# The order of the second expert turn worked out on the chip, and the last layer norm of half the rows placed among the short expert slots

## The chip, the cores and the metric

The kernel runs on one core of a Trainium2 chip. The number that is compared is the device time of the whole program in microseconds (us); each run has one time, and a kernel's time is the median of its runs. A profile is one further execution, recorded by the hardware profiler: its span runs from the first to the last instruction.

The core has TensorE (PE, matmuls; "PEld" is its weight load), VectorE (DVE), ScalarE (ACT), GpSimd (POOL) and SyncE (SP). SP and POOL issue nearly all of the DMAs here. An engine takes its instructions strictly in order: one that waits holds all that stand behind it.

## The reference

One attention layer and one mixture of experts, each followed by a layer norm, on x of shape (4, 1024, 256): 4 batch elements of 1024 tokens.

```python
x = layernorm(x + attention(x))                     # 16 heads of 16, causal
scores = (x @ router_w.T + router_b) / temp
gates  = sinkhorn(scores)                           # 3 rounds over experts and tokens of an element
topk_vals, topk_idx = top_k(gates, 2)
topk_gates = topk_vals / (topk_vals.sum(-1) + 1e-8)
g = relu(einsum('btd,edf->btef', x, wg))            # 8 experts, 256 -> 512
p = einsum('btd,edf->btef', x, wp)
all_out = einsum('btef,efd->bted', g * p, wo)       # 512 -> 256
x = layernorm(x + sum of the 2 chosen outputs, each times its gate)
```

For the given inputs the router gives the 8 experts 476, 472, 478, 516, 533, 481, 598 and 542 pairs (token, expert) from the first two elements, and 952, 937, 945, 1020, 1051, 995, 1219 and 1073 from all four (worked out from the reference).

## The kernel before

The attention of element b runs beside the projections of element b + 1 and the routing (`route`) of element b - 1. Routing is sparse: each pair is written by an indirect DMA into a list in DRAM, `pairs`, which has a region for each expert (`scatter`, L848). `base` holds each expert's next free row. An entry has the row to gather, the row to add to, and the gate.

The experts then run in *slots*. The first turn is 8 slots of 512 rows, one for each expert in the order 0 to 7; it needs only the pairs of the first three elements and starts before the last element is routed. The second turn is 8 more slots of 512 rows, the experts in the order 7 to 0, with the next 512 pairs of each; it waits for the last pairs. Its first slot takes the split weights of the slot before it (`second[0].like = first[-1]`), as that is the same expert. Then come `SURE` = 3 short slots of 256 rows for what is left over, with the expert and the place of the list read from a table that `lay_out` made; each such number is a register load on SP (`value`). Were more than three short slots filled, a conditional block would run the rest; here three are filled, so it is skipped.

What a slot does: `pairs_of` loads its entries, `gather` has POOL fetch 4 (or 2) blocks of 128 rows of x1 by indirect DMA into `xg`, `rows` turns them over on PE and splits them into a high and a low part (`split`: ACT makes the high part, DVE the low one), `weights` loads wg, wp and wo (512 KB each) on SP, `halves` splits them, and `slot` does the matmuls, three for each product (`mm3`). At its end ACT scales each 128-row block by its gate into `eo`, and POOL adds it to DRAM, `results`, by an indirect DMA that accumulates (L1039). The adds of a slot wait for the adds of the slot before it to have landed, since two experts may add to one row (`added`, `after`). `results` holds x1 from the start, so x + expert_out is there when all adds have landed. `begin(keys, n)` prepares slot n in pieces while slot n - 1 runs.

After the last slot everything is waited for. Then SP loads all of `results` in 8 pieces of 512 rows (L1255), and each piece gets its layer norm: DVE takes mean and variance (L1269, L1270), POOL makes the factor and the offset (L1272 to L1276), and the rows are scaled by ACT (first 5 pieces, L1279) or by DVE (the last `DZ` = 3, L1287) and stored (L1258).

The order of the instructions of each engine is made by a scheduler when the program is built, from the order of the calls and from a timeline of its own.

Of the kernel before, what the change touches and what calls it, by code (L numbers as in the profile page):

```python
# [9 lines left out]
F32 = mybir.dt.float32  # L10
# [13 lines left out]
DZ = 3  # L24
HB = 6
SURE = 3
# [15 lines left out]
def kernel(  # L42
# [40 lines left out]
    REGION = BT + SR  # L83
    NOVER = (2 * BT - 4 * ER + 2 * (SR - 1)) // SR
# [101 lines left out]
    def split(hi, lo, src, sub=None):  # L186

        nc.scalar.copy(hi, src)  # L188
        (sub or nc.vector).tensor_tensor(lo, src, hi.bitcast(F32), ALU.subtract)  # L189
# [495 lines left out]
    def route(b):  # L685
# [141 lines left out]
        nc.vector.tensor_tensor(base, base, ps[:, NE : NE + E], ALU.add)  # L827
        if b == B - 2:
            nc.vector.tensor_tensor(base, base, floor, ALU.max)
# [36 lines left out]

    def lay_out():
# [36 lines left out]
        nc.vector.tensor_copy(tables["filled"], upto[:, E - 1 :])  # L904
# [3 lines left out]
    def value(r, s, top):  # L908
        return nc.values_load(
            tables["slots"][0:1, r, s : s + 1], engines=[mybir.EngineType.SP], min_val=0, max_val=top,  # L910
            skip_runtime_bounds_check_because="worked out on the chip from counts that add up to 2 * B * T",
        )
# [10 lines left out]
    class Slot:  # L923


        def __init__(self, which, s):
            self.which, self.s, self.name = which, s, f"{which}_{s}"
            self.rows = SR if which == 2 else ER
            self.blocks = self.rows // P
            self.raw, self.hl = [None] * 3, [None] * 3  # L930
            self.like = None
# [3 lines left out]
    def pairs_of(k):  # L935
        if k.which == 2:
            row = value(1, k.s, NLIST - SR)
            k.ent = const.tile([P, k.blocks, 4], I32, name=f"ent_{k.name}")
            nc.sync.dma_start(
                out=k.ent, in_=pairs[bass.ds(row, SR)].rearrange("(p j) w -> p j w", j=k.blocks)  # L940
            )
            return
        if k.which not in lists:
# [6 lines left out]
            if not k.which:  # L950
                apart("pairs", "early", ins, ("last",))
        k.ent = lists[k.which][:, k.s]

    def gather(k):
        k.xg = early.tile([P, ER // P, C], F32, tag="xg", name=f"xg{k.name}", bufs=XG)
        for j in range(k.blocks):
# [3 lines left out]
            )  # L960
            if not k.which:
# [9 lines left out]
    def weights(k, i):  # L971

        if k.like is not None:
            return
        if k.which == 2:
            if i == 0:
                k.e = value(0, k.s, E - 1)
            rows_e = bass.ds(k.e, 1)
        else:
            rows_e = slice(k.s, k.s + 1)  # L980
# [4 lines left out]
    def halves(k, i):  # L985
        if k.like is not None:
            k.hl[i] = k.like.hl[i]
            return
# [16 lines left out]
    def slot(k, between):  # L1005
# [3 lines left out]
        for f in range(NFC):  # L1009
# [14 lines left out]
            split(hh, hlo, r)  # L1024
            hs.append((hh, hlo))
            next(between, None)
            if k in first[E - 3 : E - 1]:
                places.give(1.0)
        mine = []
# [85 lines left out]
    second = [Slot(1, e) for e in reversed(range(E))]  # L1115
    second[0].like = first[-1]
# [80 lines left out]
    for gen in (finish(B - 1, (0,), alone=True), route(B - 1), lay_out()):  # L1197
        drain(gen)
    filled = nc.values_load(
        tables["filled"][0:1, 0:1], min_val=0, max_val=NOVER,  # L1200
# [26 lines left out]
    def run(keys, given=()):  # L1227
        drain(begin(keys, 0, given))
        for n, key in enumerate(keys):
            slot(key, begin(keys, n + 1, given))  # L1230
            if key is first[E - 2]:
                places.until(f"S{B - 1}")

    run(first + second + further[:SURE], (0,))
# [7 lines left out]


    zp = ctx.enter_context(tc.tile_pool(name="zp", bufs=1))
    y_rows = out.rearrange("b t c -> (b t) c")
    zs = {}

    def rows_of(of, i, cut=slice(0, BPQ)):

        return of[i * QC : (i + 1) * QC].rearrange("(p n) c -> p n c", p=P)[:, cut]  # L1250

    def load_z(i):
        z = zp.tile([P, CC, FF], F32, tag="z", name=f"z{i}", bufs=BT // QC)
        z = zs[i] = z.rearrange("p k f -> p (k f)").rearrange("p (n c) -> p n c", c=C)
        nc.sync.dma_start(out=z, in_=rows_of(results, i))  # L1255

    def store_z(i, z, cut=slice(0, BPQ)):
        nc.sync.dma_start(out=rows_of(y_rows, i, cut), in_=z[:, cut])  # L1258

    n_z = BT // QC  # L1260
    rest = []
    for i in range(n_z):
        load_z(i)
    for i in range(n_z):
        z = zs.pop(i)
        mv = small.tile([P, BPQ, 2], F32, tag="mv", name=f"mv_f{i}", bufs=2)
        for j in range(BPQ):
            st = small.tile([P, 6], F32, tag="bnst", name=f"bnst_f{i}_{j}")
            nc.vector.bn_stats(st, z[:, j, :])  # L1269
            nc.vector.bn_aggr(mv[:, j, :], st)  # L1270
        rstd = small.tile([P, BPQ], F32, tag="rstdz", name=f"rstd_f{i}", bufs=4)
        nc.gpsimd.tensor_scalar_add(rstd, mv[:, :, 1], EPS_LN / 4)  # L1272
        nc.gpsimd.tensor_tensor(rstd, rstd, neg_half, ALU.pow)
        off = small.tile([P, BPQ], F32, tag="offz", name=f"off_f{i}", bufs=4)
        nc.gpsimd.tensor_tensor(off, mv[:, :, 0], rstd, ALU.mult)
        nc.gpsimd.tensor_scalar(off, off, -1.0, None, ALU.mult)  # L1276
        if i < n_z - DZ:
            for j in range(BPQ):
                nc.scalar.activation(  # L1279
                    z[:, j, :], z[:, j, :], AF.Identity, bias=off[:, j : j + 1], scale=rstd[:, j : j + 1]  # L1280
                )
            store_z(i, z)
        else:
            rest.append((i, z, rstd, off))
# [84 lines left out]
```

## Time and profile before

| | |
|---|---|
| three runs | 1086.51, 1090.79, 1091.84 us; median 1090.79 |
| the profiled execution | 1095.9 us, span 1094.2 us, mean granted TensorE clock 0.957 |
| PE busy | 975.8 us, 89% of the span |
| DVE, ACT, POOL busy | 734.9, 625.4 and 479.1 us |
| DMA | 119.67 MB, 109 GB/s over the span |

The share of PE is an average over stages. Busy time by stage, from the view by windows: in 700 to 860 us (first turn) PE is busy for 150.2 of 160 us, in 860 to 900 us for 25.5 of 40, in 900 to 1020 us (second turn) for 119.3 of 120, in 1020 to 1060 us (end of the second turn and short slots) for 36.5 of 40, and in 1060 to 1094 us for none. The gap at 860 us lies between the turns, where the list of pairs has to be complete; the 34 us at the end are the last adds and the layer norm.

### The profile page before, as it was taken

The numbers are of one execution on the slowest core, as the hardware profiler recorded it, in microseconds if no ns is written. First come the engines' busy times: TensorE is split into PE (matmuls) and PEld (weight loads), VectorE is DVE, ScalarE is ACT, GpSimd is POOL, SyncE is SP. The second block draws the span as 40 slices with busy tenths as digits, with TensorE's granted clock in tenths as the row PEclk, the third lists the DMA queues.
The fourth block names the chain that finished last, engine by engine and source line by source line (L and its number), as shares of the span: only waits on it lengthen the run. The fifth ranks groups of instructions, "written<-read, shape, count | busy, mean of one in ns | idle before, by whom it ended". The sixth has DMA issues, their size and how long they took to land.

```text
span 1094.2 us, 18114 instructions
## 1 busy us (share of the span) xinstructions
PE 975.8 (89%) x6436; PEld 608.2 (56%) x6436; DVE 734.9 (67%) x1622; ACT 625.4 (57%) x1314; POOL 479.1 (44%) x543
## 2 busy tenths in 40 slices
PE   6689999999999999989999996899999399999970
PEld 4555433455544455543444443488888288888860
DVE  4767787888888778787757882286686145555536
ACT  3445666765665755666656663656565145555533
POOL 6177511022352632552223215427557655554535
PEclk9889999999989999999999998999999699999985
DMA  6574420231240330333143220357555345656537
GB/s 245 165 213 121 117 86 18 76 117 33 95 121 17 107 114 5 127 80 98 47 102 98 46 70 2 99 174 186 141 125 123 69 109 113 172 113 164 123 36 307
DMA packets 71363, 119.67 MB, mean 109 GB/s; under 512 B 16416, under 2 KB 43040, under 8 KB 70880
## 3 DMA queue, kind: packets, MB, share of 16 engines
q1 hardware_dynamic: 48544, 81.76, 24.3%
q0 software_dynamic: 20672, 36.41, 15.5%
q8 instruction: 53, 0.87, 0.3%
q10 hardware_dynamic: 2048, 0.27, 0.2%
q14 instruction: 46, 0.38, 0.1%
HBM read 82.52 MB, written 35.60 MB: 108 GB/s over the span
## 4 chain that ended last, share of the span: by engine, by line
PE 74%; DMA 7%; DVE 6%; ACT 5%; SPq 4%; issue 2%; POOL 2%; another core or an unknown queue 1%; ACTq 0%; POOLq 0%; DVEq 0%
PE y L436 12%; PE s L351 11%; PE sT L456 10%; SPq L336 3%; PE gp L197 3%; PE gp L196 3%; PE gp L195 3%; PE eo L197 3%; PE eo L196 3%; PE eo L195 3%; PE po L625 3%; PE lp L197 2%; PE lp L196 2%; ACT pT L467 2%; PE lp L195 2%
## 5 line engine op out<-in xcount | busy, mean ns | idle before, releaser
L467 ACT ACTIVATE pT<-sT 128x512 f32<-128x512 f32 (+1 forms) x608 | 327.1, 575 | 180.8 <-PE sT L456 129.2
L372 DVE TENSOR_REDUCE mx<-s 128x1 f32<-128x384 f32 (+3 forms) x352 | 216.6, 633 | 36.2 <-PE s L368 35.1
L351 PE MATMUL s<-ks,qs 96*128 96x512 bf16 (+3 forms) x768 | 212.4, 333 | 19.4 <-DMA ks<-parts 10.8
L456 PE MATMUL sT<-qs,ks 98*128 98x512 bf16 (+3 forms) x768 | 215.5, 330 | 9.0 <-ACT pT L467 6.9
L381 DVE TENSOR_REDUCE mx<-s 128x1 f32<-128x512 f32 x256 | 171.4, 682 | 47.6 <-PE s L351 47.1
L474 POOL TENSOR_SCALAR_AFFINE_SELECT pT<-pT 128x512 f32<-128x512 f32 x112 | 70.7, 638 | 254.9 <-ACT pT L467 250.4
L436 PE MATMUL y<-pT,va 128*32 128x512 f32 (+3 forms) x1536 | 169.2, 503 | 4.4 <-ACT pT L467 3.1
L1039 POOL DMA_INDIRECT results<-eo,ents x64 | 107.2, 1674 | 82.6 <-ACT eo L1038 65.4
L351 PEld LDWEIGHTS <-qs 96*128 96x128 bf16 x768 | 70.8, 99 | 120.3 <-issue 89.7
L456 PEld LDWEIGHTS <-ks 98*128 98x128 bf16 x768 | 69.8, 99 | 89.6 <-issue 57.4
L848 POOL DMA_INDIRECT pairs<-ent,so_i x64 | 67.8, 1060 | 75.9 <-ACT pT L467 57.5
L368 PE MATMUL s<-mask,ident_b 128*128 128x128 bf16 (+2 forms) x352 | 87.1, 248 | 0.0
L1020 DVE TENSOR_TENSOR relu<-relu,lp 128x512 f32<-128x512 f32 x64 | 43.7, 683 | 60.1 <-ACT relu L1019 30.6
L195 PE MATMUL eo<-wh,hh 128*128 128x256 f32 x280 | 80.5, 289 | 0.9 <-ACT eo L1038 0.6
L957 POOL DMA_INDIRECT xg<-x_rows,ents x64 | 65.1, 1017 | 33.6 <-issue 16.1
L196 PE MATMUL eo<-wl,hh 128*128 128x256 f32 x280 | 79.0, 284 | 0.0
L189 DVE TENSOR_TENSOR wl<-w,wh 128x512 fp32r<-128x512 f32 x108 | 69.3, 684 | 14.3 <-ACT wh L188 13.8
L197 PE MATMUL eo<-wh,hl 128*128 128x256 f32 x280 | 77.7, 284 | 0.0
L1019 ACT ACTIVATE relu<-gp 128x512 f32<-128x512 f32 (+1 forms) x76 | 42.7, 563 | 59.6 <-PE gp L197 49.9
L436 PEld LDWEIGHTS y<-pT,va 128*32 128x32 f32 x1536 | 31.8, 108 | 64.6 <-issue 46.5
L195 PE MATMUL gp<-xh,wh 128*128 128x512 f32 (+1 forms) x176 | 65.0, 376 | 2.1 <-ACT xh L188 1.2
L196 PE MATMUL gp<-xl,wh 128*128 128x512 f32 (+1 forms) x176 | 65.6, 374 | 0.0
(213 smaller groups left out, 1849.0 us busy)
## 6 DMA issues: line engine op xcount, KB each, us to landing
ks<-parts SPq DMA_DIRECT2D x90, 128.0 KB
w<-in_wg_dram SPq DMA_DIRECT2D x18, 512.0 KB
w<-in_wp_dram SPq DMA_DIRECT2D x18, 512.0 KB
w<-in_wo_dram SPq DMA_DIRECT2D x18, 512.0 KB
qs<-parts SPq DMA_DIRECT2D x66, 128.0 KB
parts<-lv POOLq DMA_DIRECT2D x12, 384.0 KB
parts<-lv POOLq DMA_DIRECT2D x24, 192.0 KB
xh<-in_x_t_dram SPq DMA_DIRECT2D x8, 512.0 KB
```

Source lines behind the costliest of these rows:

```text
L195: nc.tensor.matmul(ps, lhsT=sh, rhs=mh, start=(i == 0), stop=False)
L196: nc.tensor.matmul(ps, lhsT=sh, rhs=ml, start=False, stop=False)
L197: nc.tensor.matmul(ps, lhsT=sl, rhs=mh, start=False, stop=(i == n - 1))
L351: nc.tensor.matmul(ps, lhsT=q(h, half)[:NROW, t * P : (t + 1) * P], rhs=k(h, kc)[:NROW, :w], start=first, stop=last,)
L368: nc.tensor.matmul(each[:, :, w - P :], lhsT=ident_b, rhs=mask.unsqueeze(1).to_broadcast([P, m, P]), start=False, stop=True,)
L372: nc.vector.tensor_reduce(mx_of[:, half, h0 : h0 + m, t], each, AX.X, ALU.max)
L381: nc.vector.tensor_reduce(mx_of[:, kc, h, t : t + 1], ps, AX.X, ALU.max)
L436: nc.tensor.matmul(acc[g, qc][SLOT * h : SLOT * (h + 1), lo:], lhsT=va[b % 2][:, kb, at : at + SLOT], rhs=pT[:, h, lo:], start=(kb == 0), ...
L456: nc.tensor.matmul(st[:, h % m * w : (h % m + 1) * w], lhsT=k(h, kb // BPQ)[: NROW + 2, kb % BPQ * P : (kb % BPQ + 1) * P], rhs=q(h, qc)[: ...
L467: latest[0] = nc.scalar.activation(pT[:, h + 1 - m : h + 1, lo:], st[:, : m * w].rearrange("p (h t) -> p h t", t=w), AF.Exp, scale=scale,)
L474: diagonal[0] = nc.gpsimd.affine_select(out=block, in_=block, pattern=[[0, HG], [1, P]], compare_op=ALU.is_ge, fill=0.0, base=0, channel_m ...
L1039: ins = nc.gpsimd.indirect_dma_start(out=results[:, :], out_offset=bass.IndirectOffsetOnAxis(ap=k.ent[:, j, 1:2], axis=0), in_=eo, in_offs ...
```

## The change

Four things:

1. `order_of_second`, called in the routing of the second element, finds the expert with the fewest pairs from the first two elements and makes a table `second`: experts and list places for the second turn, in rotating order, so that this expert comes last. It also makes a flag, `again`, which sends the program into the conditional block if any expert has over 1024 pairs from these two elements. The second turn's slots now read expert and place by `value` on SP, load their entries one slot at a time, and the first of them loads and splits weights of its own.
2. An expert with at most 512 pairs from the first two elements has none of them in its second slot. So the rows of `results` of the first two elements are complete when the last but one slot of the turn has been added. `load_early` loads them, 4 pieces of 512 rows, by POOL, in the last slot of the turn, after those adds have landed.
3. Their layer norm is done by DVE beside the short slots: `center_early` (mean, variance, and the factor on POOL) for pieces 0 and 1 after the first short slot's last split, `end_early` for them and `center_early` for 2 and 3 after the second's, `end_early` for 2 and 3 after the third's. SP stores them.
4. At the end only 4 pieces are left, 2 of them scaled by ACT and `DZ` = 2 by DVE.

The conditional block, when it runs, does pieces 0 to 3 again.

```diff
-DZ = 3
+DZ = 2
...
+    EARLY = B // 2
...
         nc.vector.tensor_tensor(base, base, ps[:, NE : NE + E], ALU.add)
+        if b == EARLY - 1:
+            order_of_second()
...
+    def order_of_second():
+        few = tab("few", [E])
+        nc.vector.tensor_tensor(few, floor[:1], base[:1], ALU.subtract)
+        most, again = tab("most", [1]), tab("again", [1])
+        nc.vector.tensor_reduce(most, few, AX.X, ALU.min)
+        nc.vector.tensor_scalar(again, most, -float(ER), float(NOVER), ALU.is_lt, ALU.mult)
+        tables["again"] = again
+        nc.vector.tensor_reduce(most, few, AX.X, ALU.max)
+        nc.vector.tensor_scalar(few, few, most, None, ALU.is_equal)
+        nc.vector.tensor_tensor(few, few, rank[:1], ALU.mult)
+        nc.vector.tensor_reduce(most, few, AX.X, ALU.max)
+        seq = tab("seq", [2, E])
+        seqi = tables["second"] = small.tile([1, 2, E], I32, tag="seqi", name="seqi", bufs=1)
+        nc.vector.tensor_scalar(seq[:, 0], slot_no[:, :E], most, float(E + 1), ALU.subtract, ALU.add)
+        nc.vector.tensor_copy(seqi[:, 0], seq[:, 0])
+        nc.vector.tensor_single_scalar(seqi[:, 0], seqi[:, 0], E - 1, ALU.bitwise_and)
+        nc.vector.tensor_copy(seq[:, 0], seqi[:, 0])
+        nc.vector.tensor_scalar(seq[:, 1], seq[:, 0], float(REGION), float(ER), ALU.mult, ALU.add)
+        nc.vector.tensor_copy(seqi[:, 1], seq[:, 1])
...
-        nc.vector.tensor_copy(tables["filled"], upto[:, E - 1 :])
+        nc.vector.tensor_tensor(tables["again"], tables["again"], upto[:, E - 1 :], ALU.add)
+        nc.vector.tensor_copy(tables["filled"], tables["again"])
...
     def pairs_of(k):
-        if k.which == 2:
-            row = value(1, k.s, NLIST - SR)
+        if k.which:
+            row = value(k.table, 1, k.s, NLIST - k.rows)
...
     def weights(k, i):
-        if k.like is not None:
-            return
-        if k.which == 2:
+        if k.which:
             if i == 0:
-                k.e = value(0, k.s, E - 1)
+                k.e = value(k.table, 0, k.s, E - 1)
...
-    def slot(k, between):
+    def slot(k, between, ahead=None):
...
-            split(hh, hlo, r)
+            k.mark = split(hh, hlo, r)
...
+        if ahead is not None:
+            ahead()
...
-    second = [Slot(1, e) for e in reversed(range(E))]
-    second[0].like = first[-1]
+    second = [Slot(1, n) for n in range(E)]
...
+    def load_early():
+        for i in range(n_early):
+            z = work.tile([P, T], F32, tag="yT0", name=f"ze{i}", bufs=2) if i < 2 else work.tile(
+                [P, BPQ, C], F32, tag="x1", name=f"ze{i}", bufs=X1_BUFS
+            )
+            z = early_z[i] = z.rearrange("p (n c) -> p n c", c=C) if i < 2 else z
+            with tc.issue_after(further[0].gathered.ins):
+                ins = nc.gpsimd.dma_start(out=z, in_=rows_of(results, i))
+            for o in added:
+                after(ins, o)
+    def center_early(i):
+        mv = small.tile([P, BPQ, 2], F32, tag="mve", name=f"mv_e{i}", bufs=n_early)
+        for j in range(BPQ):
+            st = small.tile([P, 6], F32, tag="bnst", name=f"bnst_e{i}_{j}")
+            nc.vector.bn_stats(st, early_z[i][:, j, :])
+            nc.vector.bn_aggr(mv[:, j, :], st)
+        rstd = small.tile([P, BPQ], F32, tag="rstdz", name=f"rstd_e{i}", bufs=4)
+        nc.gpsimd.tensor_scalar_add(rstd, mv[:, :, 1], EPS_LN / 4)
+        nc.gpsimd.tensor_tensor(rstd, rstd, neg_half, ALU.pow)
+        early_z[i] = early_z[i], mv, rstd
+    def end_early(i):
+        z, mv, rstd = early_z[i]
+        for j in range(BPQ):
+            nc.vector.tensor_scalar(
+                z[:, j, :], z[:, j, :], mv[:, j, 0:1], rstd[:, j : j + 1], ALU.subtract, ALU.mult
+            )
+        store_z(i, z)
...
-            slot(key, begin(keys, n + 1, given))
+            slot(key, begin(keys, n + 1, given), ahead.get(n))
+            with tc.issue_after(key.mark.ins):
+                for step, i in behind.get(n, ()):
+                    step(i)
...
+    run(keys, (0,), {n: load_early}, {
+        n + 1: [(center_early, i) for i in range(half)],
+        n + 2: [(end_early, i) for i in range(half)] + [(center_early, i) for i in range(half, n_early)],
+        n + 3: [(end_early, i) for i in range(half, n_early)],
+    })
...
-    for i in range(n_z):
-        load_z(i)
-    for i in range(n_z):
+    for i in range(n_early, n_z):
+        zs[i] = zp.tile([P, BPQ, C], F32, tag="z", name=f"z{i}", bufs=n_z - n_early)
+        nc.sync.dma_start(out=zs[i], in_=rows_of(results, i))
+    for i in range(n_early, n_z):
         if i < n_z - DZ:
...
+            by_scalar(i, zs[i], "f")
         else:
...
+            rest.append((i, zs[i], *norm_z(i, zs[i], "f")))
```

`by_scalar` and `norm_z` hold what the loop over the pieces did before; `n` is the place of the last slot of the second turn, `n_early` is 4.

## The prediction, as it was made before the result was known

> **What bounds the kernel now.** By the busy shares it is PE, at 89%. By stage, from the view by windows, PE is busy for 119.31 of the 120 us of the second turn, and for nothing in the last 34 us; what the change removes lies there. The chain of waits, in order of time, says what the end is made of:
>
> ```profile
> 1054.44 3.69 DMA results<-eo,ent
> ...
> 1058.95 8.45 DMA results<-eo,ent
> ...
> 1068.04 0.34 SPq L1255
> ...
> 1068.90 6.47 DMA z<-results
> 1075.46 0.49 DVE bnst_f L1269 x2
> ```
>
> The columns are start, length, what. The adds of the second short slot are issued at 1054.44 and land, those of the third at 1058.95 and land; then the loads of `results` go out at 1068.04, and the first of two waits of DVE on them ends at 1071.33, the second at 1075.46. So the end is two queues in a row: the adds, then the layer norm. The first is read in POOL's timeline (start, length, instruction, and in brackets its idle time and who ended it):
>
> ```profile
> 1022.15 2.08 POOL L1039 DMA_INDIRECT results<-eo,ents  x1 [1.25 <-ACT eo L1038]
> 1027.90 1.54 POOL L1039 DMA_INDIRECT results<-eo,ents  x1 [3.67 <-DMA results<-eo,ents]
> 1029.75 1.01 POOL L957 DMA_INDIRECT xg<-x_rows,ent  x1 [0.30 <-PE gp L197]
> ...
> 1036.61 2.08 POOL L1039 DMA_INDIRECT results<-eo,ents  x1 [0.31 <-ACT relu L1019]
> 1043.56 1.78 POOL L1039 DMA_INDIRECT results<-eo,ent  x1 [4.87 <-ACT hh L188]
> 1047.25 1.54 POOL L1039 DMA_INDIRECT results<-eo,ent  x1 [1.91 <-ACT eo L1038]
> 1051.85 1.55 POOL L1039 DMA_INDIRECT results<-eo,ent  x1 [3.06 <-ACT relu L1019]
> 1054.44 1.54 POOL L1039 DMA_INDIRECT results<-eo,ent  x1 [1.04 <-ACT eo L1038]
> 1058.95 1.55 POOL L1039 DMA_INDIRECT results<-eo,ent  x1 [2.97 <-DMA results<-eo,ent]
> 1060.81 1.55 POOL L1039 DMA_INDIRECT results<-eo,ent  x1 [0.30 <-issue]
> ```
>
> 1022.15 is the last add of the last but one slot of the second turn, 1027.90 the first of its last slot: it waited for the former to land. 1043.56 and 1047.25 are the first short slot's, 1051.85 and 1054.44 the second's, 1058.95 and 1060.81 the third's. At 1051.85 and 1058.95 an add waits for a landing, at 1043.56, 1047.25 and 1054.44 for ACT's `eo`. The latency from an issue's end to the next slot's add is 3.06 us (1048.79 to 1051.85) and 2.97 (1055.98 to 1058.95).
>
> The DMA engines, by windows of 1 us (last columns: clock, busy share of the DMA engines, GB/s):
>
> ```profile
> 1028.00:1029.00 1.00, 1.00 (x11) 1.00 (x10) 0.00 (x0) 0.58 (x2) 1.00 (x1) 1.00 1.04 351
> ...
> 1030.00:1031.00 1.00, 1.00 (x11) 1.00 (x10) 0.82 (x3) 0.89 (x3) 0.76 (x1) 1.00 1.11 271
> ...
> 1075.00:1076.00 1.00, 0.00 (x0) 0.00 (x0) 0.54 (x2) 0.87 (x2) 0.84 (x3) 0.50 1.04 410
> ```
>
> They are full from 1026 to 1031 us with the short slots' weights, and full again in the tail. The last view is DVE's timeline:
>
> ```profile
> 1038.07 0.43 DVE L189 TENSOR_TENSOR hl<-relu,hh 128x256 fp32r<-128x256 f32 x1
> ...
> 1047.51 1.29 DVE L189 TENSOR_TENSOR wl<-w,wh 128x512 fp32r<-128x512 f32 x2 [0.46 <-issue]
> ...
> 1078.36 0.36 DVE L1270 BATCH_NORM_AGGREGATE mv_f<-bnst_f 128x2 f32<-128x6 f32 x4
> ...
> 1089.35 1.38 DVE L1287 TENSOR_SCALAR z<-z,rstd_f,off_f 128x256 f32<-128x256 f32 x4 [0.67 <-POOL off_f L1276]
> ```
>
> **The tail, minus 8.0 us.** With 4 pieces the loads and the statistics of the first four stand as they are now: the fourth's are done at 1078.72 (the third line above). POOL's fourth set starts at 1079.14, has 0.23 + 1.04 + 0.20 + 0.23 us of work, and without the next piece's add between ends at 1081.28. DVE's four scalings (1.38 us, last line) end at 1082.70, not at 1090.73: 8.03 us. Behind them lie the last store and its landing (1090.73 to the span's end, 3.47 us), as now. ACT's two pieces are done by 1079.8 (2.07 us, then 8 of the 16 scalings that take 7.97 us from 1077.81). Bounds: 7.1, if the store queue still sets the end (2.1 MB from 1077.3 at 262 GB/s, the mean of the last 6 us, lasts until 1085.3, and 1.8 us passed now between the engines' falling quiet at 1092.4 and the end), and 9, if less traffic also brings the third piece earlier and takes its 0.89 us wait away.
>
> **The adds, plus 4.8 us.** `load_early` stands on POOL where the add of 1027.90 stood, and waits for the same landing. Its four issues cost 0.88 + 3 x 0.80 = 3.3 us (the seven stores of x1 from POOL: median 0.878, then 0.787). Behind them in POOL's queue: the gather of the third short slot (2.6 us), then the four adds of the turn's last slot. These write `results`, which the loads read, so in the compiled order the first of them waits for all four loads. It went at 1027.90; now it goes when 2.1 MB have landed. First bytes come 1.5 us after the issue (store issued at 239.4, engines busy from 240.9): 1029.4. In the tail the loads had their first bytes at 1069.0, the third piece landed at 1075.46, and the fourth follows 1.3 us later at 410 GB/s: 7.7 us. Add 1.0 us for some 0.35 MB of weights still under way (0.67 MB move from 1029.4 to 1032, of which 0.26 are the gather's): 1038.1. Bounds: 1035.4 (2.1 MB at 350 GB/s) and 1040.8 (at 184 GB/s, the row of 1036 to 1040).
>
> From there I follow the queue. The four adds at a pitch of 1.95 (now 1.92 and 2.34) end at 1045.6 and land at 1048.6. First short slot: 1048.6 instead of 1043.56. Now POOL has `rstd` of pieces 0 and 1 in its order before this add and the next, 0.23 and 1.05 us each with gaps of 0.08 (1.4 us): the second add goes at 1051.9. Plus landing: 1056.5, second short slot; its second add, behind one more `rstd` step, at 1058.65; landing 1063.2, third slot; last add 1065.0 instead of 1060.81. Two `pow` of pieces 2 and 3 (2.5 us) fit into the last landing's 2.97. That is plus 4.2.
>
> DVE comes to nearly the same place by another way. Its stats of pieces 0 and 1 stand before the second short slot's work and find their data landed (wait free: 1038.5, against a first piece by about 1033). But the scaling of piece 1 waits for the `rstd` that POOL does behind the first short slot's add: 1051.6. Behind it in DVE's order stand 1.4 us of scaling, 1.41 of stats, the split of wo (1.29 us, which ran at 1047.51), then the third slot's products: the last `hl` ends at 1061.4, PE's last 15 matmuls at 0.12 us and ACT's two `eo` follow, and the last add is ready at 1065.1. If PE, idle for about 4 us by then, runs at half clock (it did at 1039 to 1042, granted clock 0.50, after being busy for 1.4 of the 3 us before), it is 1066.5. I take plus 4.8. Bounds: with the loads' landing from 1035.4 to 1040.8, plus 1.5 to plus 8. The stores of the early pieces and DVE's scaling of 2 and 3 (2.8 us after 1061.4) end before the last add lands; if not, they would be waited for, 1 us at most.
>
> The Trainium skill speaks against an early load here ("DMA: Bandwidth & Descriptors", "Issuing engines are not separate DMA queues"): a transfer issued from another engine runs on the same 16 DMA engines and interleaves with what is under way. The rows agree, since the share is 1.0 from 1026 to 1031 us; by the rule taken fully, the loads would share with all that the weights have left at 1028 (1.57 MB less the 0.76 moved since 1024), not with 0.35 MB, and the sum would be 1.3 us worse. The same page's fit for DMAs from GpSimd ("Anatomy of one DMA — SWDGE (gpsimd) path", 2.0 us plus bytes over 436 GB/s) gives as an estimate 6.8 us for the 2.1 MB, and a sum 2.5 us better; no run here shows that fit.
>
> **Between the turns, plus 0.5 us.** Now the weights of the second slot of the turn are loaded by 840 us. After the change their load stands on SP behind the entries' loads, which wait for the last pairs (864.53); entry, two register loads and the second entry (1.13 us as between the two L946 and L939 issues), so wg goes out at 866.8, wp at 867.4. On ACT and DVE their splits stand before the `xh` and `xl` of the turn's first slot, which start at 875.18 and 875.80. At 1.9 us for each 512 KB, with 3.3 us for the first (1068.04 to 1071.33), wp lands at 872.1, ACT's two casts (1.13) end at 873.2: hidden. The cover is 2.0 us. Entries for one expert instead of eight may land up to 1 us sooner, the gathers may share the engines and land 1 to 2 later. The slot's 6 extra splits and 1.5 MB take the place of those that stood there a slot later; in the turn itself, SP's register loads and entry loads run a slot ahead of the gather, and nothing waits. Bounds -1 and +13 (rival 2).
>
> **The small tables, plus 0.3 us.** 13 DVE instructions on one partition at 511 us (and one more in `lay_out`), at 0.15 us as the copies and sums of `lay_out`: 2.0 us. DVE had 13.3 busy of 20 us there and PE 18.0, so most is cover; bounds 0 and 2.2.
>
> **Sum.** -8.0 + 4.8 + 0.5 + 0.3 = -2.4 us on the profiled execution, 1095.9, so 1093.5. It lay 5.1 us over the median of the runs, 1090.79; the same difference there gives **1088.4**. All bounds on one side give 1082 and 1096 (rival 2 left out); being independent, 1084 to 1093.
>
> **Rivals.** *1, the adds catch up.* POOL's 10.9 us of idle time between 1038.69 and 1054.44 is slack: if the loads land by 1034 and the order on POOL does not matter, the adds end with ACT's `eo` as now, plus 1. Then -8.0 + 1 + 0.8: 1084.6. For it: the slack is real. Against: landing chains of 3 us stand in it, and the loads need 7.7 us alone.
>
> *2, the gap between the turns grows.* The weights that now follow the list land late, and ACT and DVE hold the gathered rows behind them. It decides once wp lands after 874.1. The price: 1.57 MB at 117 GB/s, the rate while gathers run at 870 us, from 868.3 is 13.4 us, 881.7, which is 7.6 too late; at 83 GB/s, the mean of 860 to 900, 18.9 us and 13.1 too late. In place of the 0.5 the sum is plus 4.7 to plus 10.2: 1095.5 to 1101, middle 1098. For it: SP's order is plain, and PE is idle there, so each us counts. Against: while gathers run the share of the DMA engines is only 0.3 to 0.4 (the DMA view's slices of 868 to 878 us).
>
> *3, the conditional block runs.* 22 further slots of about 10 us (1043.56 to 1051.85 to 1058.95 in POOL's lines give 7 to 8 for a short slot): over 150 us more. The counts exclude it: at most 598 pairs, and the flag needs over 1024; three short slots fill.
>
> **Chances.** Forecast 0.58, rival 1 0.25, rival 2 0.12, rival 3 0.01; 0.04 for small slips beyond these. A measurement of this kernel tells 0.5% (5.4 us) from no change: its three runs spread over 5.3 us. Faster by more: 0.26 (rival 1 and the forecast's edge); within: 0.59; slower: 0.15 (rival 2 above 1096.2, 0.09; its rest of slips and the forecast's upper edge, 0.06). The range takes in rival 1's lower side and the forecast's upper bounds with half of rival 2: 1082.5 to 1096.
>
> **What would show it.** The loads `ze` issued near 1028 and landing near 1038; the turn's last adds right after; the last add near 1065; the tail from the first load of `z` to the end near 18 us instead of 26.2; PE's gap between the turns as before. The forecast is wrong if the last add stays near 1061 (rival 1), or if the second turn's first matmul slips by over 3 us (rival 2).

## The result, and the profile after

The changed kernel takes 1096.12 us (median of 6 runs, 1093.55 to 1098.21), the kernel before beside it 1089.85: a ratio of 1.0062, 95% interval 1.0043 to 1.0081, so 6.8 us slower where 2.4 us faster was forecast, and just beyond the upper end of the range. (Where a ratio is given in us below, it is the ratio times the median of the kernel before beside it.) The profiled execution took 1094.95 us (span 1093.2), less than that of before (1095.9), so totals of the two profiles mislead: before the experts' first matmul, where the programs differ by the small tables alone, they are 5.8 us apart (708.4 against 702.6), the other way. I count from that matmul. Three stretches, in us:

| profile | experts' first matmul to the second turn's first | from there to the issue of the last add | from there to the end | sum |
|---|---|---|---|---|
| before | 167.4 | 185.0 | 33.4 | 385.8 |
| before, a second profile | 166.8 | 182.5 | 32.1 | 381.4 |
| after | 168.8 | 195.3 | 26.5 | 390.6 |
| after, a second profile | 169.7 | 194.3 | 28.3 | 392.4 |

The end is shorter, as forecast, and the adds lose more than that. POOL's timeline of the changed kernel (start, length, instruction, idle time before it and who ended it):

```profile
1018.05 3.29 POOL L1064 DMA_INDIRECT results<-eo,ent  x1 [1.25 <-ACT eo L1063]
1026.79 2.35 POOL L1296 DMA_DIRECT2D ze<-results  x4 [5.44 <-DMA results<-eo,ent]
...
1038.75 1.62 POOL L1064 DMA_INDIRECT results<-eo,ent  x1 [6.37 <-ACT xh L190]
...
1044.48 1.53 POOL L1064 DMA_INDIRECT results<-eo,ent  x1 [0.30 <-ACT wh L190]
...
1048.98 1.63 POOL L1064 DMA_INDIRECT results<-eo,ent  x1 [1.53 <-ACT relu L1042]
...
1052.22 1.75 POOL L1064 DMA_INDIRECT results<-eo,ent  x1 [0.20 <-issue]
1057.96 1.55 POOL L1064 DMA_INDIRECT results<-eo,ent  x1 [3.99 <-ACT hh L190]
...
1059.97 1.58 POOL L1064 DMA_INDIRECT results<-eo,ent  x1 [0.18 <-ACT relu L1042]
...
1064.58 1.77 POOL L1064 DMA_INDIRECT results<-eo,ent  x1 [0.50 <-ACT eo L1063]
1066.66 1.55 POOL L1064 DMA_INDIRECT results<-eo,ent  x1 [0.30 <-POOLq L1339]
```

The second turn began 4.4 us earlier here than in the profile of before (871.38 against 875.82), so 4.4 goes onto each time before it is set beside the forecast. 1018.05 is the last add of the last but one slot. Its issue took 3.29 us (2.08 before), and the early loads waited 5.44 us for it to land (3.67 before): they go out at 1031.2 in the time of before, where 1027.9 was forecast. 12.0 us after they begin, the first add of the last slot goes (10.2 forecast). Behind it, all is nearly as forecast: 27.9 us to the last add (27.5). The windows of 2 us show the loads' time (last columns: clock, busy share of the DMA engines, GB/s):

```profile
1022.00:1024.00 2.00, 2.00 (x20) 2.00 (x19) 0.00 (x0) 0.00 (x0) 0.00 (x0) 1.00 1.05 204
...
1034.00:1036.00 2.00, 0.81 (x7) 0.60 (x5) 1.79 (x8) 0.38 (x1) 0.00 (x0) 1.00 1.01 382
1036.00:1038.00 2.00, 0.63 (x4) 0.47 (x5) 0.00 (x0) 0.00 (x0) 0.00 (x0) 1.00 0.56 197
1038.00:1040.00 2.00, 2.00 (x20) 2.00 (x19) 1.56 (x6) 1.31 (x4) 1.25 (x1) 1.00 0.00 1
```

The engines are full with weights already at 1022, ahead of the loads, and quiet when the add goes at 1038.75. PE (first busy column) falls to 0.63 of 2 us: it waits 2.5 us for the rows of the third short slot, whose gather stands behind the loads in POOL's queue.

```profile
1037.31 0.69 PE L1025 MATMUL xgT_ps<-ident,xg 128*128 128x128 f32 x2 [2.50 <-DMA xg<-x_rows,ent]
```

DVE's timeline shows the wait for `rstd` that the forecast named, PE's the one behind it, and the windows the half clock that the forecast held possible (0.50 ahead of the last two columns):

```profile
1052.06 1.50 DVE L1315 TENSOR_SCALAR ze<-ze,mv_e,rstd_e 128x256 f32<-128x256 f32 x4 [3.19 <-POOL rstd_e L1309]
```
```profile
1056.51 0.58 PE L197 MATMUL gp<-xh,wh 128*128 128x256 f32 x1 [5.98 <-DVE relu L1043]
```
```profile
1056.00:1058.00 2.00, 1.49 (x7) 1.49 (x8) 2.00 (x11) 1.38 (x4) 0.04 (x1) 0.50 0.45 89
```

Last, SP's queue: stores of the early pieces, the loads of z, and what SP waited for between 1050 and 1080 us (total, times, longest).

```profile
1064.07 1.79 SPq L1260 DMA_DIRECT2D out_dram<-ze  x2
1074.33 1.76 SPq L1356 DMA_DIRECT2D z<-results  x4
```
```profile
SPq L1339 <- SPq L1339: 6.3, 2, 4.6
```

Line 1339 is the conditional block. The loads come 6.1 us after the last add's issue ends (1068.21), with 5.7 before; from the first load to the end it is 18.8 us (26.2 before; 18 forecast).

### The profile page after: what moved, and what is told of

It is laid out like the page before. It is cut to its first block, busy times and chain, and to the rows that moved or that the text cites. A ratio compares the mean times of both kernels' runs of the same rounds, so it can differ in the third digit from the quotient of the medians.

```text
span 1093.2 us, 18209 instructions
## 1 busy us (share of the span) xinstructions
PE 978.2 (89%) x6436; PEld 610.8 (56%) x6436; DVE 744.0 (68%) x1654; ACT 621.7 (57%) x1308; POOL 481.9 (44%) x539
## 5 line engine op out<-in xcount | busy, mean ns | idle before, releaser
L191 DVE TENSOR_TENSOR wl<-w,wh 128x512 fp32r<-128x512 f32 x114 | 73.3, 684 | 30.4 <-ACT wh L190 27.7
L1064 POOL DMA_INDIRECT results<-eo,ent x38 | 64.3, 1692 | 46.0 <-ACT eo L1063 18.9
L190 ACT CAST wh<-w 128x512 fp32r<-128x512 f32 x114 | 63.9, 617 | 21.5 <-DMA w<-in_wg_dram 14.3
L1064 POOL DMA_INDIRECT results<-eo,ents x32 | 55.0, 1719 | 36.0 <-ACT eo L1063 26.8
```

Of the source, the lines that this page charges most:

```text
L191: return (sub or nc.vector).tensor_tensor(lo, src, hi.bitcast(F32), ALU.subtract)
L1064: ins = nc.gpsimd.indirect_dma_start(out=results[:, :], out_offset=bass.IndirectOffsetOnAxis(ap=k.ent[:, j, 1:2], axis=0), in_=eo, in_offs ...
```

## The experiments

Each kernel was timed in turns with the kernel before on the same chip. That one's median was 1078 to 1089 us from one set of runs to the next, so only ratios compare. "Stretch" means a column of the table above; each profile is one execution.

One thing has to be kept apart when stretches are compared. In ten of the 20 profiles the last add of the last but one slot took about 3.3 us to issue and landed late; in the others it took 2.1 us or less. Two profiles of one kernel, the order alone, show both:

```profile
1018.35 3.28 POOL L1064 DMA_INDIRECT results<-eo,ent  x1 [1.25 <-ACT eo L1063]
1027.25 1.54 POOL L1064 DMA_INDIRECT results<-eo,ent  x1 [5.62 <-ACT relu L1042]
```
```profile
1014.44 2.07 POOL L1064 DMA_INDIRECT results<-eo,ent  x1 [1.26 <-ACT eo L1063]
1020.30 1.54 POOL L1064 DMA_INDIRECT results<-eo,ent  x1 [3.79 <-DMA results<-eo,ent]
```

With a late landing, what waits for it begins 154 us or more after the second turn's first matmul, otherwise at 150 to 152.5. The kernels without early loads have a second stretch of 181.9 to 185.0 (six profiles, mean 183.3) with an early landing and of 184.1 to 185.7 (five, mean 185.2) with a late one: slack hides about half of the 3.5 us. I say "early" and "late" of a profile in this sense. What makes a landing late is open.

**What the parts cost.** The order alone: no early steps, all 8 pieces at the end, three on DVE.

```diff
-    run(keys, (0,), {n: load_early}, {...})
+    run(keys, (0,))
...
-    for i in range(n_early, n_z):
+    for i in range(n_z):
```

> The second turn in the worked-out order, with entries and weights of its own, but no early loads and the layer norm of all 8 pieces at the end, as before. Theory A (the loss is the adds' wait for the early loads): the order itself costs 0.3 to 1 us, so 0 to +1 us against before. Rival B (the order costs it: gap between the turns, entries and weights of each slot): +4 to +6 us, the same loss as the whole change.

Ratio 1.0035 (1.0021 to 1.0049), +3.8 us: between the theories, nearer to rival B. Its stretches are 168.4, 185.5 and 32.3 (a late profile): only the first is clearly longer than before, by 1.0.

The tail alone: the same `run(keys, (0,))`, with the tail of 4 pieces left as in the changed kernel.

> The worked-out order and the short tail of 4 pieces; the first 2048 rows of the output are left out, with their loads, norm and stores. Theory A: the tail is worth what the changed kernel's trace shows, 6.7 us, less at most 1 for the order: -5.5 to -6.5 us against before. Rival B: -6.7 + 5, so -1 to -2 us.

0.9962 (0.9946 to 0.9978), -4.1 us: again between the theories. Against the order alone that is 0.73%, 7.9 us, for half the tail; the profiles have 24.1 and 32.3, 8.2. The forecast of 8.0 holds for the tail by itself.

The loads alone:

```diff
-    run(keys, (0,), {n: load_early}, {...})
+    run(keys, (0,), {n: load_early})
```

> As the changed kernel, with the four early loads, but without their statistics, scalings and stores (the first 2048 rows of the output are left out). Theory A: the adds of the turn's last slot wait for the loads as in the changed kernel, about 12 us, and the last add is within 1 us of its place there: +3 to +6 us against before. Rival C (VectorE's work and the rstd steps in POOL's queue hold the adds): most of the loss goes, -4 to 0 us.

1.0057 (1.0040 to 1.0074), +6.2 us, just above what theory A gave. From the tail alone it differs by the loads and nothing else, and that costs 10.3 us of time, 7.6 in the second stretch (193.0 against 185.4, both late). Its POOL timeline:

```profile
1029.92 2.35 POOL L1296 DMA_DIRECT2D ze<-results  x4 [5.43 <-DMA results<-eo,ent]
...
1041.47 1.63 POOL L1064 DMA_INDIRECT results<-eo,ent  x1 [5.98 <-issue]
```

11.6 us from loads to add with no statistics, no `rstd` and no scaling in the program: rival C falls as the main cause. The norm adds 1.3 to 2.3 us to that stretch (194.3 and 195.3 against 193.0, all late).

**The wait taken away.** With these inputs the adds behind the loads touch none of the loaded rows, so the dependence can be dropped:

```diff
+            if k is second[-1] or k in further[:SURE]:
+                apart("results", "add", ins, ("norm",))
...
+            apart("results", "norm", ins, ("add",))
```

> As the changed kernel, but the adds behind the early loads (the turn's last slot, the short slots) are declared to touch other rows, so they do not wait for the loads to land. Theory A: the first of the adds goes some 4 us after the loads' issue starts instead of 12, the last add comes 5 to 9 us sooner, and the kernel is at -2 to -6 us against before. Rival C: the adds still stand behind the norm's steps, and it stays at +3 to +6 us.

The time is 1.0034 (1.0016 to 1.0052), +3.7: a miss of theory A by time, and what rival C gave. The second stretch is 185.7, but this profile is an early one. The order alone has 183.2 early, so some 2.5 us of loss remain there, about POOL's issue of the four loads. The last stretch grew to 28.4, where the tail alone has 24.1. POOL's and SP's timelines of that run:

```profile
1022.30 2.35 POOL L1298 DMA_DIRECT2D ze<-results  x4 [3.69 <-DMA results<-eo,ent]
1024.96 1.80 POOL L1064 DMA_INDIRECT results<-eo,ent  x1 [0.30 <-ACT hh L190]
...
1055.68 1.55 POOL L1064 DMA_INDIRECT results<-eo,ent  x1 [0.30 <-issue]
```
```profile
1065.26 1.76 SPq L1359 DMA_DIRECT2D z<-results  x4
```

The add follows the start of the loads' issue after 2.7 us, not 12; but the loads of z go out 8.0 us after the last add's issue ends (1057.23). In the run of the tail alone it is 4.1 us (1064.10 to 1068.21), and there SP had passed the block and stood at the loads:

```profile
SPq L1352 <- DMA results<-eo,ent: 25.4, 1, 25.4
```

With the early stores in its queue SP cannot: it stores, waits at the block's end, then loads. Two runs test that. First, with these stores issued by ScalarE (`nc.scalar.dma_start` in place of `store_z` in `end_early`):

> As the run with the adds declared apart, but the stores of the early pieces are issued from ScalarE's queue instead of SP's. Theory F (SP comes to the branch of the conditional block only behind these stores, and the loads of z wait for the branch, not for the last add): the first load of z goes 4 to 5 us after the end of the last add's issue instead of 8, and the kernel is 3 to 4 us faster than that run, -1 to +1 us against before. Rival G (the stores' own traffic, or the landing of the last add, holds the loads): no change, +3 to +4 us against before.

1.0035 (1.0010 to 1.0059): no gain. The loads of z go 4.3 us after the last add's issue ends and the last stretch fell to 26.1, but the second is 191.3, in a late profile. ACT now waits for DVE's scalings ahead of its last `eo`, but that wait does not set the last add: the `eo` is done at 1054.59, and the add goes at 1055.80, straight behind the one before it. Then with the stores of pieces 2 and 3 behind the loads of z, and the block writing these pieces back into their tiles:

```diff
+        if i < n_early // 2:
             store_z(i, z)
...
+    for i in range(half, n_early):
+        store_z(i, early_z[i][0])
```

> As the run with the adds declared apart, but the stores of early pieces 2 and 3 stand in SP's queue behind the loads of z, after the conditional block, which writes these two pieces back to the same tiles instead of storing them. Theory F (the end of the conditional block waits on SP for the early stores to land, then jumps, and only then do the loads of z go): the first load of z goes 4 to 5 us after the end of the last add's issue instead of 8, the kernel gains 2 to 4 us on that run, -1 to +1.5 us against before. Rival G (the stores' traffic costs the same wherever it stands): no gain, +3 to +4 us.

The loads go 4.5 us after the last add and the last stretch is 24.7, 3.7 less than with the adds apart alone: theory F stands in both profiles. The time does not show it, 1.0048 (1.0018 to 1.0078). The second stretch is 191.1 here, late again: the loads had waited until 155.1 us after the turn's first matmul, against 152.3 in the first of these three runs.

So where the landing is late, dropping the dependence leaves 191.1 and 191.3, against 194.3 and 195.3 with it and 185.4 and 185.5 without early loads: it takes away 3 to 4 of the 9 to 10 us (these kernels differ in where the early stores go, too). Something else holds the short slots there, and PE's timeline of the last run shows what comes first:

```profile
1028.54 0.30 PE L1025 MATMUL xgT_ps<-ident,xg 128*128 128x128 f32 x1 [3.41 <-DMA xg<-x_rows,ent]
```
```profile
1030.00:1032.00 2.00, 2.00 (x12) 2.00 (x11) 2.00 (x7) 0.68 (x3) 1.53 (x3) 0.50 0.58 68
```

PE waits 3.4 us (4.3 in the run before) for the rows of the third short slot, whose gather stands behind the late loads in POOL's queue, and the granted clock then falls to 0.50. In the early profile that wait is 0.9 us. Later the second short slot's first add goes 5.3 us after the issue of the add before it ended, where the early profile has 2.9. How the remaining loss divides between PE's wait and the landing of the adds was not tested.

**Where the loads stand.** Behind the third add of the last slot, with all early stores behind the loads of z:

```diff
-    run(keys, (0,), {n: load_early}, {
+    run(keys, (0,), {n + 1: load_early}, {
```

> The adds declared apart as before, but the early loads are issued behind the third of the four adds of the turn's last slot instead of ahead of the first, the early statistics start one short slot later, and all four early stores stand behind the loads of z. Theory A: now nothing of the adds waits for the loads or for their issue: from the second turn's first matmul to the last add 183 to 187 us (with the early issue 185.7 to 191.3, in the changed kernel 194 to 195), from the last add to the end 24 to 27, and the kernel is at -4 to -1 us against before, if the order and the tables cost 3. Rival J (the short slots are slowed by the early norm itself, wherever the loads stand): 190 us or more to the last add, and +2 to +5 us against before.

1.0064 (1.0039 to 1.0089), +7: a miss, with stretches of 168.3, 190.8 and 29.9 in an early profile. POOL's timeline:

```profile
1024.25 2.84 POOL L1305 DMA_DIRECT2D ze<-results  x4
1027.39 1.64 POOL L1068 DMA_INDIRECT results<-eo,ent  x1 [0.30 <-issue]
1036.36 1.58 POOL L1068 DMA_INDIRECT results<-eo,ent  x1 [7.32 <-issue]
```

The next slot's first add goes 7.3 us after the issue of the fourth ends, with its `eo` done at 1029.5. By the trace the fourth add, issued behind the loads, has landed at 1035.5, 6.5 us after its issue ended, where the other adds of that run that the trace shows take 2.2 to 3.3. And the norm, begun later, ended at 1061.4, which held the loads of z. Rival J is not excluded here, since steps of `rstd` keep POOL busy from 1044.2 to 1047.3, when it goes on to the next add.

Loads from ScalarE's queue, then from SP's, all else as in the run with two stores behind:

```diff
-                ins = nc.gpsimd.dma_start(out=z, in_=rows_of(results, i))
+                ins = nc.scalar.dma_start(out=z, in_=rows_of(results, i))
```

> As the run with the adds apart and two stores behind the loads of z (e9), but the early loads are issued from ScalarE's queue, so they stand in another queue than the adds. Theory K (an add that is issued behind the early loads in GpSimd's queue lands only behind their 2.1 MB): the adds of the last slot land some 3 us after their issue again, 183 to 187 us from the second turn's first matmul to the last add (e9: 191.1), and -3 to +1 us against before. Rival L (the 16 DMA engines are full, whatever the queue): 190 us or more, +3 to +5 us.

> The same from SP's queue, where the loads stand among the short slots' weights: theory K gives the adds the same 183 to 187 us unless the weights behind the loads come late; then the third short slot's matmuls start later than 168 to 170 us after the second turn's first, and the kernel is at +2 to +5 us against before. Rival L: 190 us or more.

From ScalarE: stretches 169.1, 185.3 and 25.6, a time of 0.9983 (0.9961 to 1.0005), 1.9 us under the kernel before: the best of all versions that compute everything, though not clear of no change. From SP: second stretch 189.3, ratio 1.0021 (1.0000 to 1.0042); the third short slot's last transposes came at 173.6 us, not 168.4. There ACT waited 5.7 us for the slot's weights and PE 4.8 us for its rows, as the loads of its weights and of its list entries stand behind the early loads in SP's queue. Both profiles are early ones. ScalarE's run in POOL's timeline:

```profile
1024.59 1.54 POOL L1064 DMA_INDIRECT results<-eo,ent  x1 [3.79 <-DMA results<-eo,ent]
...
1033.45 1.55 POOL L1064 DMA_INDIRECT results<-eo,ent  x1 [0.30 <-ACT xh L190]
...
1042.29 1.64 POOL L1064 DMA_INDIRECT results<-eo,ent  x1 [2.86 <-ACT hh L190]
```

The adds start with nothing ahead of them, yet the next slot's first add again goes 7.3 us after the last one's issue ends (1035.00 to 1042.29), with the engines full to 1038; a wait for ACT ends it, so not all of the 7.3 us need be the landing. By the trace the add of 1024.59, with nothing ahead of it in its queue, has landed only at 1033.6, 7.5 us after its issue ended. So theory K (a shared queue delays the landing) is not needed: full engines do as well, and the 185.3 came without the landing in 3 us that the theory named. Against the early profile with the adds apart and the loads on POOL (185.7) the second stretch gains 0.4 us. By time ScalarE's queue gains more, 0.65% or 7 us against the run that differs by the queue alone (1.0048). It fits that the gather no longer stands behind the loads, whose wait swings; but no late profile of this kernel was taken, so that is not shown.

**The small tables.** The tables alone, in the kernel before, three times; the kernel before against itself; and the order with 12 of the 13 instructions moved to the end of the layout.

```diff
+        if b == B // 2 - 1:
+            order_of_second()
```

> The kernel before with nothing added but the small tables (order_of_second at 511 us); the turn's order stays as it was. Theory D (the 13 instructions stand in VectorE's queue in the middle of attention and cost about what the order alone cost): +2.5 to +4 us against before. Rival E (the order costs at its steps in the second turn, or the +3.7 us of the order alone came of other things): 0 to +0.8 us.

> The run with the tables alone once more, on whatever chip this is. If its cost is one of the kernel: +2 to +4.5 us against before again. If it was chance, or of that chip: 0 us within 1.2.

> The tables alone for the third time, beside the run with spare instructions on one chip: +2 to +4 us against before if its cost is one of the kernel, 0 us within 1.2 if the first two (+3.6 and +1.9) were chance.

> The kernel before, unchanged, as a measure of the comparison itself and for a second profile of it: 0 us within 1.5. In the profile the experts' first matmul near 699 to 702 us instead of 708.4, and 384 to 387 us from there to the end, as in the first profile (385.8).

> As the run with the order alone, but only one of the tables' instructions (the difference of counts) stays at 511 us; the others stand behind the short slots' tables, at the end of the layout. Theory D: most of the order's cost goes, 0 to +1.2 us against before. Rival E: it stays, +3 to +4 us.

The tables: 1.0033 (1.0009 to 1.0056), 1.0018 (0.9991 to 1.0045), 1.0012 (0.9986 to 1.0037). The kernel before against itself: 1.0005 (0.9987 to 1.0024); its second profile missed both figures expected of it, with the experts' first matmul at 696.3 and 381.4 us from there. The order with late tables: 1.0053 (1.0026 to 1.0081), so moving them away from 511 us brought no gain. Nor does the profile show it there. These are POOL's stores of x1 ahead of the tables and after them, in the second profile of before, then in the first run of the tables:

```profile
440.62 0.89 POOL L653 DMA_DIRECT2D x_rows<-x  x1 [2.02 <-DVE x L555]
547.63 0.90 POOL L653 DMA_DIRECT2D x_rows<-x  x1 [0.76 <-DVE nm L393]
```
```profile
437.55 0.89 POOL L653 DMA_DIRECT2D x_rows<-x  x1 [2.01 <-DVE x L555]
544.53 0.90 POOL L653 DMA_DIRECT2D x_rows<-x  x1 [0.77 <-DVE nm L393]
```

107.01 us without the tables, 106.98 with them. Two runs with spare instructions in the kernel before, 14 of DVE on one partition, at the start and behind the first turn's last product:

> The kernel before with 14 small instructions of VectorE on one partition at the start of the program, where VectorE has nothing to do; no tables. Theory H (the cost of the tables alone, +3.6, comes of the program being longer or laid out otherwise, not of the tables): +2 to +4 us against before. Rival I (it is the tables' place in the attention, or chance): 0 us within 1.2.

> The kernel before with 14 small instructions of VectorE behind its last product of the first turn, where it then has nothing to do for over 10 us; no tables. Theory H (what the tables alone cost comes of 14 more instructions in the program): +2 to +4 us against before. Rival I (it comes of their place in the attention): 0 us within 1.2.

At the start they were not free, so that run tells nothing of the theories: 1.0142 (1.0101 to 1.0183). In DVE's timeline 13 of them take 17.4 us, and what stands behind them starts 10.7 us late. They are not alike: the first three take 3.4 to 3.5 us each, beside POOL's first large fills, the last four 0.16. The second line has their least, median and greatest length in ns:

```profile
2.24 17.37 DVE L161 TENSOR_SCALAR spare<-spare 1x16 f32<-1x16 f32 x13
```
```profile
L161 DVE TENSOR_SCALAR spare<-spare x13: 161/542/3530, 2.2 to 19.4; 1x16 f32<-1x16 f32 x13
```
```profile
2.24 10.47 POOL L177 MEMSET ks<- 2x4096 bf16 x3
```

In the gap (0.16 us each there, in the median) they cost 1.0006 (0.9984 to 1.0028), on the chip where the tables gave 1.0012. And the order alone once more, on that chip:

> The order alone once more, beside the tables alone on one chip: the order's own steps (entries, weights and the gap between the turns) should add 1 to 2 us to the tables alone, as the stretch from the experts' first matmul to the second turn's first (168.0 to 169.8 against 166.7 to 167.4) says; if not, they are hidden.

1.0037 (1.0014 to 1.0060): 0.25%, 2.7 us, more than the tables there, with the first stretch at 168.2 against 167.6; the two intervals overlap.

One trace of the tables does show in the profiles. All ten late profiles are of kernels with the tables (ten of 16), and all four of kernels without them are early. A late landing costs about 1.9 us in the second stretch where there are no early loads, so it may be a part of what the tables cost. With one profile of most kernels, that is a guess, not shown.

The changed kernel once more:

> The changed kernel once more, for a second profile. Theory A: +5 to +7.5 us against before; from the second turn's first matmul to the last add 193 to 196 us as in the first profile (195.3; before 182.5 and 185.0), from the last add to the end 26 to 27 (26.5; before 32.1 and 33.4). If those two stretches differ by over 1.5 us from the first profile, its sum is not to be trusted.

1.0113 (1.0071 to 1.0154), +12.2 (9.4 between the medians), more than expected. The adds' stretch is near that of the first profile (194.3); the last is 28.3, 1.8 longer, with the loads of z 7.9 us behind the last add's issue. By the words set down for this run, the first profile's sum is then not to be trusted to its last us.

## Why the prediction was wrong, by its steps

- **The tail, -8.0.** Right by itself: 7.9 by time, 8.2 in the profiles. In the changed kernel it was 6.9 (33.4 to 26.5), and 3.8 in the second profiles (32.1 to 28.3). The clause that failed here stands at the end of the adds' step: the early stores "end before the last add lands; if not, they would be waited for, 1 us at most". The loads of z came 2.0 and 3.8 us later behind the last add than with the tail alone. I had looked at the transfers and not at what SP passes on its way: the end of the conditional block, which SP used to pass while the adds were under way.
- **The adds, +4.8, bounds +1.5 to +8.** This is the step that failed: +10.3 (195.3 against 185.0), and +11.8 in the second profiles. The path is the one named: the first add waits for all four loads, the short slots follow, and DVE waits for `rstd` behind them. The mis-sized term is the landing, twice: the loads went out 3.3 us later than forecast, as the landing ahead of them was late, and the add followed 12.0 us after, not 10.2; the queue behind it took 27.9 us, not 27.5. I took the landing ahead of the loads from one profile (an idle time of 3.67 us); in the ten late profiles it is 5.1 to 6.3. Kernels without early loads pay about half of such a lateness too (185.2 against 183.3); late beside late, the adds still lose 9 to 10 us (194.3 and 195.3 against 185.4 and 185.5).

  That the early loads cause the loss is shown by the loads alone, 10.3 us dearer in time than the tail alone. That the adds' wait is its path is shown in part: without that wait 2.5 us remain in an early profile, and nearly 6 in late ones, where the gather behind the loads holds PE first. This second path the forecast had at nothing: it counted the gather behind the loads as 2.6 us of POOL, and not that the third slot's rows would be late.

  The prediction had a warning: the Trainium skill ("DMA: Bandwidth & Descriptors", "Issuing engines are not separate DMA queues") has transfers of all issuing engines interleave on the same 16; the share of 1.05 ahead of the loads agrees, and to share with all of the weights, which I priced at 1.3 us and did not take, would have been nearer. Its further sentence, that issuing elsewhere saves the sequencer's time alone, agrees with the two early profiles (185.3 from ScalarE, 185.7 from GpSimd); the 7 us by time are more than the 2.4 us of issue. The four issues took 2.4 us, not 3.3, which changes no term.
- **Between the turns, +0.5.** In its bounds: from the first turn's last matmul to the second's first 21.4 became 21.8, in the second profiles 21.2 and 23.0. The first turn took 1.0 us more than before (147.0 against 146.0), of which the forecast said nothing.
- **The small tables, +0.3, bounds 0 to 2.2.** Open. The 13 instructions took 2.95 us of DVE in the changed kernel, not 2.0. Three measurements lie at 1.3 to 3.6 us, only the first clear of nothing; the profile shows no cost at the place; 14 spare instructions elsewhere give 0.6. The order with its tables costs 3.8 and 4.0 us by time, of which the profiles show 0.8 to 1.6, in the first stretch. I can't name the rest.
- **The sum.** By the profiles 10.3 - 6.9 + 1.4 = +4.8, by the second ones +11.0 (392.4 against 381.4), by time +6.8 (4.7 to 8.8) and +12.2 (7.7 to 16.6). The rivals: that the adds catch up is refuted, as the engines are quiet only at 1038, which is 1042 in the time of before, not at 1034; the gap between the turns did not grow as rival 2 had it; the conditional block was not entered.

## What to carry to other kernels

A load moved ahead of queued work is paid for by what waits for its landing, not by its own length: find the first instruction in the queue that must wait for it, and how much slack the chain behind it has. A wait whose length swings from run to run, and that slack hides in part today, must be priced at its long end once the slack is spent. Look at everything that stands behind the load in its queue, and not only at what waits for its data: here a gather of rows was held as well. Compare profiles only where such a wait is of the same length in both. Ask of each queue what it passes early today (here the end of a branch), and whether something new now stands ahead of that.

## What the runs showed of the hardware

- 13 dependent instructions of DVE on 16 elements took 0.16 to 3.5 us each (542 ns in the median) from 2 to 20 us, the longest beside POOL's fills from 2.24 to 12.71, and 0.16 us each (median) at 846 us. That the fills are the cause was not tested.
- In 19 of the 20 profiles one indirect add, always the last of the last but one slot, took either about 2.1 us to issue, with 3.0 to 3.9 us behind it until the next instruction that waits for it (nine profiles), or 3.3 us, with 5.1 to 6.3 (ten). In the other one it stands in another order.
- Two profiles of one unchanged program lie 12.1 us apart at the experts' first matmul (708.4 and 696.3); all 20 profiles range from 688.7 to 709.9. A part is windows of half clock that come at one time and not at another: over all profiles, between the layer norms stored at 271 and 406 us, 132.9 to 134.2 us with 3.4 us of half clock and 134.5 to 135.5 with 6.8. Of the 12.1 us, 2.0 lie between the stores at 440 and 550 us (109.1 with 3.4 us of half clock, 107.0 with none). Most of the rest is not explained by it.
